# A selective scan's input products shared with GpSimd, and one ScalarE table for Exp and Ln

## Chip, core and metric

One NeuronCore of a Trainium2 chip. The time is that of one execution on the device, in microseconds (us).

## What is computed

Four images of 256 channels and 64 x 64 points go through four layers, each `x = x + layer(groupnorm(x))`: a deformable convolution, a self-attention, a second deformable convolution with groups, and a state-space layer (Mamba). The change is in the last one, layer 3, whose core is this (512 inner channels, 16 states, 4096 points in a row):

```python
delta = softplus(dt @ dt_proj_w.T + dt_proj_b)
deltaA = exp(delta * A)                 # A = -exp(A_log), per channel and state
deltaBu = delta * B * u                 # B per point and state
state = deltaA * state + deltaBu        # step by step along the points
y = sum over states of state * C        # C per point and state
out = ((y + u * D) * silu(res)) @ out_proj_w.T
```

## The kernel before

The images follow one another, each through layers 0 to 3. Layer 3 (`layer3`) cuts the 4096 points into 8 chunks of `C = 512`; the 512 channels lie in four groups (`dc`) of 128 partitions. A chunk has `DS = 16` states, so an image has 128 steps of the loop over `s`, with `j` the chunk and `n` the state. Everything is float32 but the two operands of `bn`.

One state:

- TensorE spreads row n of B over all partitions into PSUM (`bn`, L1396, one bank for all states).
- VectorE multiplies `du` (delta times u) by `bn`, 128 x 2048 elements, into `h` (L1468).
- ScalarE makes `da = exp(delta * A)` for each of the four groups (L1475, two PSUM banks), and VectorE runs the recurrence over it (L1476, four scans that start from `carry`).
- GpSimd saves the last column as `carry` (L1487) and multiplies `h` by row n of C (L1490). That row, `cn`, was spread over the partitions by a DMA from a small DRAM tile `cd` (L1394, six buffers).
- TensorE adds `h` into `y` with a unit matrix (`add`, L1388), two states later.

Beside the states of one chunk, the next chunk is prepared by `front(j)`: normalised input `xn` (L1222 on ScalarE, L1220 on GpSimd for chunk 1), projections into `up` (L1190, L1194), the short convolution (`convolve`, L1236 and L1241) into `u`, the Silus of `u` and of the gates (L1250, L1206), the shares dt, B, C (L1259, `dbc` at L1263, `cd` at L1266), the softplus (L1274, Abs and Relu at L1280 and L1281, Exp at L1287, Ln at L1303, additions on GpSimd at L1296, L1305, L1306, and `du` at L1307). `close` projects the finished chunk and stores it. All projections and convolutions share one PSUM bank (`front`).

The order of TensorE, ScalarE, VectorE and GpSimd is written out by hand. Each piece of `front` has a step and a half; `front(j)` runs with step 0 at state 12 of chunk j-2 (`LEAD = 4`), so that chunk j's convolutions fall into states 14, 15, 0 and 1 and its Silus into state 2; `front(1)` runs two states later, in chunk 0. `fill` puts a piece's matmuls on TensorE's queue, `empty` the rest on ScalarE's and GpSimd's. The end of a state's step in the loop:

```python
                    empty(s, 2)
                    if s + 1 < total:
                        state((s + 1) // DS, (s + 1) % DS)
                    late.append((j, n, h))
                    if len(late) > 2:
                        add(*late.pop(0))
                    fill(s + 1, 0)
```

So on TensorE's queue `bn` of the next state stands behind the second half's piece and ahead of the `y` products. SP, which issues the DMAs, is not in the hand-written order. ScalarE's table loads are placed by the compiler ahead of a function that the loaded set does not hold.

`first` prepares chunk 0 of an image alone, ahead of the loop. The whole code, cut to what the change touches:

Of the kernel before, what the change touches and what calls it, by code (L numbers as in the profile page):

```python
# [9 lines left out]
F32 = mybir.dt.float32  # L10
I32 = mybir.dt.int32
BF16 = mybir.dt.bfloat16
AF = mybir.ActivationFunctionType
# [3 lines left out]
P = 128  # L17
# [11 lines left out]
DS = 16  # L29
# [34 lines left out]
class Net:  # L64
# [993 lines left out]
    def layer3(self, x, out, nxt, early):  # L1058
# [2 lines left out]

        nc, tc = self.nc, self.tc
        C = 512
        NC, LEAD = N // C, 4
        with (
# [17 lines left out]
            pick = pa.tile([P, DS, P], BF16, tag="pickn", name="pickn")  # L1085
# [8 lines left out]
            tail = pa.tile([P, 4, 3], F32, tag="tail", name="tail")  # L1094
            nc.gpsimd.memset(tail, 0.0)
            kept = pa.tile([P, 2, C], F32, tag="kept", name="kept")
            tiny = pa.tile([P, 1], F32, tag="tiny", name="tiny")
            chunks = [{} for _ in range(NC)]

            def bank():  # L1100
                return self.psum.tile([P, C], F32, tag="ps", name="front")

            def first():


                c = chunks[0]
                spare = lambda: py.tile([P, C], F32, tag="y", name="front")
                xn = pa.tile([P, 2, C], F32, tag="xn3", name="xn3")
                for ct in range(2):
                    nc.vector.tensor_scalar(  # L1110
                        xn[:, ct, :], x[:, ct, :C], rs[:, ct : ct + 1], shift[:, ct : ct + 1], ALU.mult, ALU.add
                    )
                up = pa.tile([P, 4, C + 3], F32, tag="up", name="up")
                nc.gpsimd.tensor_copy(up[:, :, 0:3], tail)
                u, delta, du, w = (
                    pool.tile([P, 4, C], F32, tag=n, name=n)
                    for pool, n in ((pb, "u"), (pb, "delta"), (pb, "du"), (pa, "w3"))
                )
                c.update(u=u, delta=delta, du=du)

                def project(dc):
                    pu = spare()
                    for ct in range(2):
                        nc.tensor.matmul(pu, win[:, ct, bass.ts(dc, P)], xn[:, ct, :], start=(ct == 0), stop=(ct == 1))
                    nc.vector.tensor_copy(up[:, dc, 3:], pu)

                def convolve(dc):
                    cv = spare()
                    for i in range(4):
                        nc.tensor.matmul(cv, conv[:, dc, i, :], up[:, dc, i : i + C], start=(i == 0), stop=(i == 3))  # L1130
                    nc.scalar.activation(u[:, dc, :], cv, AF.Silu, bias=cb[:, dc : dc + 1])

                project(0)
                project(1)
                convolve(0)
                project(2)
                convolve(1)
                project(3)
                nc.gpsimd.tensor_copy(tail, up[:, :, C : C + 3])
                convolve(2)  # L1140
                convolve(3)
                px = bank()
                for dc in range(4):
                    nc.tensor.matmul(px, xpw[:, dc, :], u[:, dc, :], start=(dc == 0), stop=(dc == 3))
                nc.scalar.activation(tiny, self.eps, AF.Exp)
                dbc = pa.tile([P, C], F32, tag="dbc", name="dbc")
                nc.scalar.copy(dbc, px)
                c["cd"] = self.dram.tile([DS, C], F32, tag="cd", name="cd")
                nc.sync.dma_start(out=c["cd"], in_=dbc[16:32, :])
                pzs = []  # L1150
                for dc in range(4):
                    pzs.append(spare())
                    nc.tensor.matmul(pzs[dc], dtw[:, bass.ts(dc, P)], dbc, start=True, stop=True)

                c["gates"] = [spare() for _ in range(4)]
                for dc, pg in enumerate(c["gates"]):
                    for ct in range(2):
                        nc.tensor.matmul(
                            pg, win[:, ct, bass.ts(4 + dc, P)], xn[:, ct, :], start=(ct == 0), stop=(ct == 1)
                        )  # L1160
                bp, t = c["bp"], _ = (
                    pb.tile([P, C], BF16, tag="bp", name="bp"),
                    pa.tile([P, C], BF16, tag="bt", name="bt"),
                )
                for lo, hi in ((0, 64), (64, 96), (96, 128)):
                    nc.gpsimd.tensor_copy(bp[lo:hi], dbc[lo:hi])
                    if hi < P:
                        nc.gpsimd.tensor_copy(t[hi:], dbc[hi:])
                        nc.gpsimd.tensor_sub(dbc[hi:], dbc[hi:], t[hi:])
                for dc in range(4):  # L1170
                    nc.scalar.activation(w[:, dc, :], pzs[dc], AF.Abs, bias=dtb[:, dc : dc + 1])
                    nc.scalar.activation(du[:, dc, :], w[:, dc, :], AF.Exp, scale=-1.0)
                    nc.vector.tensor_scalar(delta[:, dc, :], pzs[dc], dtb[:, dc : dc + 1], 0.0, ALU.add, ALU.max)
                    nc.vector.tensor_scalar_add(w[:, dc, :], du[:, dc, :], 1.0)
                    nc.vector.scalar_tensor_tensor(
                        du[:, dc, :], w[:, dc, :], -1.0, du[:, dc, :], ALU.add, ALU.subtract
                    )
                    nc.vector.tensor_sub(delta[:, dc, :], delta[:, dc, :], du[:, dc, :])
                for dc in range(4):
                    nc.scalar.activation(w[:, dc, :], w[:, dc, :], AF.Ln)  # L1180
                    nc.vector.tensor_add(delta[:, dc, :], delta[:, dc, :], w[:, dc, :])
                    nc.vector.tensor_mul(du[:, dc, :], delta[:, dc, :], u[:, dc, :])
# [21 lines left out]
            def gate_silu(j):  # L1204
                sres = chunks[j]["sres"]
                nc.scalar.activation(sres, sres, AF.Silu)  # L1206

            def front(j):


                c = chunks[j]
# [37 lines left out]
                def silu():  # L1249
                    nc.scalar.activation(c["u"], c["u"], AF.Silu)  # L1250
                    gate_silu(j - 1)

                put(6, 0, None, silu)

# [6 lines left out]
                def keep():  # L1261
                    c["dbc"] = pa.tile([P, C], F32, tag="dbc", name="dbc")
                    nc.scalar.copy(c["dbc"], c["b"])  # L1263

                    c["cd"] = self.dram.tile([DS, C], F32, tag="cd", name="cd")
                    nc.sync.dma_start(out=c["cd"], in_=c["dbc"][16:32, :])  # L1266

                put(7, 1, shares, keep)

# [34 lines left out]
                last = 17 if j > 1 else 15  # L1304
# [82 lines left out]
                for dc in range(4):  # L1387
                    nc.tensor.matmul(c["ys"][dc], self.ident, h[:, dc, :], start=False, stop=(n == DS - 1))  # L1388

            def state(j, n):  # L1390

                c = chunks[j]
                cn = c["cn", n] = pb.tile([P, 1, C], F32, tag="cn", name="cn", bufs=6)
                nc.sync.dma_start(out=cn, in_=c["cd"][n : n + 1, :].unsqueeze(0).to_broadcast([P, 1, C]))  # L1394
                bn = c["bn", n] = pbb.tile([P, 1, C], F32, tag="bn", name="bn")
                nc.tensor.matmul(bn[:, 0, :], pick[:, n, :], c["bp"], start=True, stop=True)  # L1396


            slots = {}
# [10 lines left out]
                    slots.setdefault((DS * (j + 1) + step, half), []).append((pe, rest))  # L1410
            last = DS * (NC - 1)
            slots.setdefault((last, 0), []).append((None, keep))
            slots.setdefault((last + 2, 0), []).append((None, lambda: gate_silu(NC - 1)))
            slots.setdefault((last + 2, -1), []).append((None, lambda: fetch(NC - 1)))
            slots.setdefault((last + 5, -1), []).append((None, lambda: count(NC - 1)))
            for i in range(2):
# [30 lines left out]
            with tc.manual_schedule(  # L1447
# [8 lines left out]
                for pe, rest in begin:  # L1456
                    if pe:
                        pe()
                    rest()
                state(0, 0)  # L1460
                fill(0, 0)
                late = []
                total = NC * DS
                for s in range(total):
                    j, n = s // DS, s % DS
                    c = chunks[j]
                    h = pb.tile([P, 4, C], F32, tag="h", name="h", bufs=4)
                    nc.vector.tensor_mul(h, c["du"], c.pop(("bn", n)).to_broadcast([P, 4, C]))  # L1468
                    empty(s, -1)
                    if j and n == 2:  # L1470
                        gated(j - 1)
# [1 line left out]
                    def scan(dc):  # L1473
                        da = pda.tile([P, C], F32, tag="da", name="da")
                        nc.scalar.activation(da, c["delta"][:, dc, :], AF.Exp, scale=al[:, dc, n : n + 1])  # L1475
                        nc.vector.tensor_tensor_scan(  # L1476
                            h[:, dc, :], da, h[:, dc, :], carry[:, dc, n : n + 1], ALU.mult, ALU.add
                        )

                    scan(0)  # L1480
                    scan(1)
                    empty(s, 0)
                    fill(s, 1)
                    scan(2)
# [7 lines left out]
                        nc.vector.tensor_mul(h[:, 0:2, :], h[:, 0:2, :], cn.to_broadcast([P, 2, C]))  # L1492
                        nc.gpsimd.tensor_mul(h[:, 2:4, :], h[:, 2:4, :], cn.to_broadcast([P, 2, C]))
                    empty(s, 2)
                    if s + 1 < total:
                        state((s + 1) // DS, (s + 1) % DS)
                    late.append((j, n, h))
                    if len(late) > 2:
                        add(*late.pop(0))
# [131 lines left out]
```

## Time and profile before

| what | us |
|---|---|
| median of three runs (lowest, highest) | 10109.86 (10098.28, 10119.21) |
| the profiled execution | 10144.41 |
| its span, first to last instruction | 10142.6 |
| TensorE busy in the span | 8738.3 (86%) |
| VectorE busy | 7651.8 (75%) |
| GpSimd busy | 6768.8 (67%) |
| ScalarE busy | 4961.6 (49%) |
| layer 3 of image 0, first product of a state to the last | 1614.6 to 2565.8 |

The shares are means over four different layers; a layer-3 stretch of the trace has to be read by itself. In a group of instructions the columns are: line, engine, operation, output and inputs with their shapes, count, then busy time and mean ns of one, then the idle time of the engine just before them with what ended it. PE is TensorE, PEld its weight loads, DVE VectorE, ACT ScalarE, POOL GpSimd. A float32 matrix product shows as two matmuls.

### The profile page before, as it was taken

To read this page: it belongs to the slowest core of one execution; us is meant where nothing else is said; L and a number is where in the kernel's file an instruction comes from. 1 tells how busy PE (TensorE), PEld (TensorE's weight loads), DVE (VectorE), ACT (ScalarE), POOL (GpSimd) and SP (SyncE) were. 2 spreads that over 40 slices of the span, in tenths; PEclk is the share of its full clock that TensorE was granted. 3 is DMA by queue.
4 is the path that set the end of the run, shared out by engine and by line. 5 is a ranking of instruction groups with operands and counts; after the bars stand their busy time and mean duration, and the time that the engine had idled before them with its cause. 6 is when DMAs were issued, how large, how long until landed. Compare 5 with 4: busy or idle time off the path is not lost.

```text
span 10142.6 us, 88824 instructions
## 1 busy us (share of the span) xinstructions
PE 8738.3 (86%) x29189; PEld 4281.7 (42%) x29193; DVE 7651.8 (75%) x8215; ACT 4961.6 (49%) x7588; POOL 6768.8 (67%) x3952
## 2 busy tenths in 40 slices
PE   5789898998678989899877898989986789998997
PEld 3643343333464334333346434433334643443333
DVE  5764497999676459799967545889995754688998
ACT  3743334665474333566557333266645733326664
POOL 3646686787474668688757366768865736677886
PEclk9889999999899999999989999999998999999999
DMA  7830011111783001111178201111118810111111
GB/s 263 310 137 1 25 49 39 44 45 48 259 312 119 1 29 49 38 44 47 45 287 323 78 1 36 51 38 44 44 43 316 308 62 1 38 49 38 40 40 34
DMA packets 377891, 956.56 MB, mean 94 GB/s; under 512 B 34675, under 2 KB 107820, under 8 KB 375372
## 3 DMA queue, kind: packets, MB, share of 16 engines
q0 software_dynamic: 165888, 604.05, 16.6%
q1 hardware_dynamic: 211532, 346.73, 10.8%
q8 instruction: 234, 3.83, 0.2%
q14 instruction: 237, 1.94, 0.1%
HBM read 784.59 MB, written 92.32 MB: 86 GB/s over the span
## 4 chain that ended last, share of the span: by engine, by line
PE 24%; DVE 9%; ACT 5%; issue 4%; POOL 4%; DMA 3%; another core or an unknown queue 1%; SPq 0%; POOLq 0%; DVEq 0%; ACTq 0%
PE cx L555 5%; DVE h L1476 4%; PE pacc L840 3%; PE y L1388 2%; DMA g<-tab,idx 2%; PE pm L455 2%; PE front L1236 2%; POOL h L1490 2%; DVE h L1468 2%; PE sc L531 2%; PE front L1190 1%; ACT da L1475 1%; DVE r L353 1%; POOL g L344 1%; DMA ring<-ring 1%
## 5 line engine op out<-in xcount | busy, mean ns | idle before, releaser
L1476 DVE TENSOR_TENSOR_SCAN h<-da,carry,h 128x512 f32<-128x512 f32 x2048 | 2470.6, 1264 | 140.9 <-ACT da L1475 92.5
L1490 POOL TENSOR_TENSOR h<-h,cn 128x2048 f32<-128x2048 f32 x508 | 2300.0, 4527 | 41.1 <-POOL carry L1487 0.4
L1475 ACT ACTIVATE da<-delta,l3a 128x512 f32<-128x512 f32 x2048 | 1388.6, 689 | 1152.5 <-DVE h L1476 1150.7
L1388 PE MATMUL y<-h,ident 128*128 128x512 f32 x4096 | 1931.4, 616 | 4.5 <-POOL h L1490 3.5
L344 POOL DMA_INDIRECT g<-tab,idx x1152 | 1363.3, 1183 | 791.1 <-issue 362.8
L548 POOL TENSOR_TENSOR acc<-acc,e 128x1024 f32<-128x1024 f32 x480 | 1125.1, 2344 | 540.4 <-ACT e L544 519.7
L388 PE MATMUL pz<-cols,l0w 128*128 128x256 f32 x4608 | 1217.5, 411 | 219.8 <-ACT cols L377 95.8
L1388 PEld LDWEIGHTS y<-h,ident 128*128 128x128 f32 x4096 | 810.2, 198 | 1279.3 <-issue 1209.7
L353 DVE SCALAR_TENSOR_TENSOR r<-g,wx,r 128x512 f32<-128x512 f32 x1152 | 858.1, 745 | 434.3 <-ACT r L352 321.9
L1468 DVE TENSOR_TENSOR h<-du,bn 128x2048 f32<-128x2048 f32 x512 | 1157.9, 2262 | 26.3 <-PE front L1190 14.2
L465 DVE TENSOR_REDUCE m<-pm 128x3 f32<-128x1536 f32 (+1 forms) x372 | 602.3, 1625 | 716.9 <-PE pm L455 715.2
L388 PEld LDWEIGHTS pz<-cols,l0w 128*128 128x128 f32 x4608 | 896.9, 205 | 390.7 <-ACT cols L377 100.9
L823 DVE TENSOR_TENSOR prod<-ring,A 128x1280 f32<-128x1280 f32 x640 | 922.4, 1480 | 122.7 <-DMA ring<-ring 102.7
L555 PE MATMUL cx<-e,v 128*128 128x512 f32 x2048 | 1001.4, 616 | 0.0
L544 ACT ACTIVATE e<-sc 128x1024 f32<-128x1024 f32 x512 | 496.0, 1020 | 1032.4 <-PE sc L531 1032.4
L352 ACT ACTIVATE r<-g,wx 128x512 f32<-128x512 f32 x1152 | 826.6, 718 | 270.0 <-DMA g<-tab,idx 219.2
L840 PE MATMUL pacc<-prod,ident 128*128 128x512 f32 x1920 | 915.3, 610 | 37.7 <-DVE prod L823 23.7
L832 POOL TENSOR_TENSOR prod<-prod 128x512 f32<-128x512 f32 x640 | 800.3, 1274 | 187.8 <-DVE prod L823 170.1
L370 PE MATMUL pt<-ident,acc 128*128 128x128 f32 x2304 | 430.9, 295 | 304.9 <-DVE acc L361 200.7
L1487 POOL COPY carry<-h 128x4 f32<-128x4 f32 x512 | 98.0, 191 | 807.4 <-DVE h L1476 797.6
L555 PEld LDWEIGHTS cx<-e,v 128*128 128x128 f32 x2048 | 352.2, 189 | 598.8 <-issue 596.3
L360 ACT ACTIVATE acc<-r,wy 128x256 f32<-128x256 f32 x1152 | 571.4, 496 | 28.0 <-DVE r L353 22.4
(250 smaller groups left out, 11138.0 us busy)
## 6 DMA issues: line engine op xcount, KB each, us to landing
cn<-cd SPq DMA_DIRECT2D x512, 256.0 KB
tab<-vt SPq DMA_DIRECT2D x112, 640.0 KB
ring<-ring SPq DMA_DIRECT2D x288, 126.0 KB
ring<-ring SPq DMA_DIRECT2D x288, 124.0 KB
g<-tab,idx POOLq DMA_INDIRECT x1152
x<-in_x SPq DMA_DIRECT2D x64, 256.0 KB
out<-x SPq DMA_DIRECT2D x56, 256.0 KB
l0w<-in_l0w SPq DMA_DIRECT2D x4, 2304.0 KB
```

The lines of the kernel that those rows point to most:

```text
L344: nc.gpsimd.indirect_dma_start(out=g[:], out_offset=None, in_=tab[:, :], in_offset=bass.IndirectOffsetOnAxis(ap=idx[:, t, k : k + 1], axis=0),
L353: nc.vector.scalar_tensor_tensor(r, g[:, :, 1, :], wx[:, 1, t, k : k + 1], r, ALU.mult, ALU.add)
L388: nc.tensor.matmul(sums[m][:, ot, :256], wf[:, i, bass.ts(ot, P)], cols[m][:, i, :], start=(i == 0), stop=(i == 17),)
L548: nc.gpsimd.tensor_add(b["acc"], b["acc"], e)
L555: nc.tensor.matmul(blocks[qb]["cx"], v[:, 4 * (i + kt // 4 * 4) + kt % 4, :], e[:, bass.ts(i % 2, 512)], start=(kt == 0 and i == 0), stop= ...
L823: nc.vector.tensor_mul(d["prod"][:, :, t, :].rearrange("p x (g c) -> p x g c", c=GC), ring[y // VR % 4][:, :, y % VR, :].rearrange("p x (g ...
L840: nc.tensor.matmul(d["pd"], self.ident, prod[:, wx, :], start=(wy == 0 and wx == 4), stop=(wy == WIN - 1 and wx == 2),)
L1388: nc.tensor.matmul(c["ys"][dc], self.ident, h[:, dc, :], start=False, stop=(n == DS - 1))
L1468: nc.vector.tensor_mul(h, c["du"], c.pop(("bn", n)).to_broadcast([P, 4, C]))
L1475: nc.scalar.activation(da, c["delta"][:, dc, :], AF.Exp, scale=al[:, dc, n : n + 1])
L1476: nc.vector.tensor_tensor_scan(h[:, dc, :], da, h[:, dc, :], carry[:, dc, n : n + 1], ALU.mult, ALU.add)
L1490: nc.gpsimd.tensor_mul(h, h, cn.to_broadcast([P, 4, C]))
```

## The change

Three things. In states 14, 15 and 0 to 5 the fourth group's product `du * B` is made by GpSimd, a state ahead (`quarter`), from a row of B that a DMA spreads into SBUF (`bs`, two buffers); VectorE's product covers three groups there. For this `cd` holds the rows of C and of B, and `ahead` issues the loads two states ahead, `cn` with four buffers in place of six. `bn` is still made for all states. And ScalarE loads the table set that holds Exp and Ln by name (`tables`), once in `first` and after each pair of Silus.

```diff
@@ first @@
-                nc.scalar.activation(tiny, self.eps, AF.Exp)
+                tables()
...
-                c["cd"] = self.dram.tile([DS, C], F32, tag="cd", name="cd")
-                nc.sync.dma_start(out=c["cd"], in_=dbc[16:32, :])
+                c["cd"] = self.dram.tile([2 * DS, C], F32, tag="cd", name="cd")
+                nc.sync.dma_start(out=c["cd"], in_=dbc[16:48, :])
@@ front: silu, keep (cd as above) @@
                     gate_silu(j - 1)
+                    tables()
@@ layer3 @@
+            def tables():
+                nc.scalar.preload_act_table_set("natural_log_exp_and_others")
...
-            def state(j, n):
-                c = chunks[j]
-                cn = c["cn", n] = pb.tile([P, 1, C], F32, tag="cn", name="cn", bufs=6)
-                nc.sync.dma_start(out=cn, in_=c["cd"][n : n + 1, :].unsqueeze(0).to_broadcast([P, 1, C]))
-                bn = c["bn", n] = pbb.tile([P, 1, C], F32, tag="bn", name="bn")
-                nc.tensor.matmul(bn[:, 0, :], pick[:, n, :], c["bp"], start=True, stop=True)
+            hs, helped = {}, (14, 15, 0, 1, 2, 3, 4, 5)
+            def ahead(s):
+                if s < NC * DS:
+                    j, n = s // DS, s % DS
+                    c = chunks[j]
+                    for name, r, bufs in (("cn", n, 4), ("bs", DS + n, 2)):
+                        if name == "cn" or n in helped:
+                            t = c[name, n] = pb.tile([P, 1, C], F32, tag=name, name=name, bufs=bufs)
+                            nc.sync.dma_start(
+                                out=t, in_=c["cd"][r : r + 1, :].unsqueeze(0).to_broadcast([P, 1, C])
+                            )
+            def state(s):
+                if s < NC * DS:
+                    c = chunks[s // DS]
+                    bn = c["bn", s % DS] = pbb.tile([P, 1, C], F32, tag="bn", name="bn")
+                    nc.tensor.matmul(bn[:, 0, :], pick[:, s % DS, :], c["bp"], start=True, stop=True)
+            def quarter(s):
+                if s < NC * DS:
+                    c = chunks[s // DS]
+                    hs[s] = pb.tile([P, 4, C], F32, tag="h", name="h", bufs=4)
+                    if s % DS in helped:
+                        nc.gpsimd.tensor_mul(hs[s][:, 3:4, :], c["du"][:, 3:4, :], c.pop(("bs", s % DS)))
...
-            slots.setdefault((last + 2, 0), []).append((None, lambda: gate_silu(NC - 1)))
+            slots.setdefault((last + 2, 0), []).append((None, lambda: (gate_silu(NC - 1), tables())))
@@ the loop over states @@
-                state(0, 0)
+                for s in range(2):
+                    ahead(s)
+                state(0)
+                quarter(0)
...
-                    h = pb.tile([P, 4, C], F32, tag="h", name="h", bufs=4)
-                    nc.vector.tensor_mul(h, c["du"], c.pop(("bn", n)).to_broadcast([P, 4, C]))
+                    h = hs.pop(s)
+                    d = 3 if n in helped else 4
+                    nc.vector.tensor_mul(
+                        h[:, :d, :], c["du"][:, :d, :], c.pop(("bn", n)).to_broadcast([P, d, C])
+                    )
+                    ahead(s + 2)
...
                     scan(1)
+                    quarter(s + 1)
                     empty(s, 0)
...
-                    if s + 1 < total:
-                        state((s + 1) // DS, (s + 1) % DS)
+                    state(s + 1)
```

More of the change, by code (lines that the diff above doesn't have):

```diff
@@ L1096, in layer3 @@
             kept = pa.tile([P, 2, C], F32, tag="kept", name="kept")
-            tiny = pa.tile([P, 1], F32, tag="tiny", name="tiny")
             chunks = [{} for _ in range(NC)]
@@ L1263, in keep @@
                     nc.scalar.copy(c["dbc"], c["b"])
-                    c["cd"] = self.dram.tile([DS, C], F32, tag="cd", name="cd")
-                    nc.sync.dma_start(out=c["cd"], in_=c["dbc"][16:32, :])
+                    c["cd"] = self.dram.tile([2 * DS, C], F32, tag="cd", name="cd")
+                    nc.sync.dma_start(out=c["cd"], in_=c["dbc"][16:48, :])
                 put(7, 1, shares, keep)
```

## The prediction, made before the change was run

> **What bounds the kernel now.** I read the granted clock first (one core, 0.950 over the span), then the costliest groups on the page, to see what layer 3 is made of:
>
> ```profile
> L1476 DVE TENSOR_TENSOR_SCAN h<-da,carry,h 128x512 f32<-128x512 f32 x2048 | 2470.6, 1264 | 140.9 <-ACT da L1475 92.5
> L1490 POOL TENSOR_TENSOR h<-h,cn 128x2048 f32<-128x2048 f32 x508 | 2300.0, 4527 | 41.1 <-POOL carry L1487 0.4
> ...
> L1388 PE MATMUL y<-h,ident 128*128 128x512 f32 x4096 | 1931.4, 616 | 4.5 <-POOL h L1490 3.5
> ...
> L1468 DVE TENSOR_TENSOR h<-du,bn 128x2048 f32<-128x2048 f32 x512 | 1157.9, 2262 | 26.3 <-PE front L1190 14.2
> ```
>
> A state on VectorE is one product (2.26) and four scans (4.81 from first start to last end, and some 0.05 between): 7.09 us. VectorE is idle for only 26 us before 512 products and 141 us before 2048 scans, so a shorter product looks like a gain everywhere. The windows view asks who else is full. I cut a stretch of image 0 at the starts of VectorE's products; the rows are states 14 and 15 of chunk 2 (counted from 0), then 0 to 5 of chunk 3. Columns: stretch, length, busy time (count) of PE, weight loads, DVE, ACT, POOL, then granted clock, DMA share, GB/s.
>
> ```profile
> 1962.03:1969.60 7.57, 6.80 (x17) 2.86 (x16) 7.08 (x7) 2.95 (x5) 7.46 (x4) 1.00 0.21 67
> 1969.60:1976.71 7.11, 7.11 (x18) 3.13 (x17) 7.01 (x6) 3.29 (x6) 6.64 (x4) 1.00 0.02 4
> 1976.71:1983.80 7.09, 7.09 (x18) 3.13 (x17) 6.99 (x6) 3.27 (x6) 4.72 (x2) 1.00 0.21 66
> 1983.80:1990.89 7.09, 7.09 (x18) 3.13 (x17) 6.99 (x6) 3.27 (x6) 4.72 (x2) 1.00 0.16 32
> 1990.89:2001.88 10.99, 10.99 (x27) 4.85 (x26) 9.40 (x11) 9.82 (x10) 4.75 (x2) 1.00 0.11 33
> 2001.88:2008.96 7.08, 7.08 (x18) 2.94 (x16) 6.98 (x6) 3.25 (x5) 4.72 (x2) 1.00 0.11 30
> 2008.96:2016.05 7.09, 5.28 (x13) 2.21 (x13) 6.99 (x6) 4.80 (x8) 4.72 (x2) 1.00 0.12 40
> 2016.05:2023.14 7.09, 5.59 (x13) 2.01 (x12) 6.99 (x7) 5.02 (x9) 4.72 (x2) 1.00 0.14 36
> ```
>
> In states 15, 0 and 1 **TensorE is as full as VectorE**. A busy PE need not be at its peak, so I read the start times in the timeline:
>
> ```profile
> 1972.76 3.60 PE L1236 MATMUL front<-up,conv 128*128 128x512 f32 x8
> 1976.19 0.38 PE L1396 MATMUL bn<-bp,pickn 128*128 128x512 bf16 x1
> 1976.41 3.60 PE L1388 MATMUL y<-h,ident 128*128 128x512 f32 x8
> 1979.84 3.60 PE L1236 MATMUL front<-up,conv 128*128 128x512 f32 x8
> ```
>
> Eight matmuls take 3.43 from start to start, `bn` 0.22: 3.43 + 3.43 + 0.22 = 7.08 a state, back to back. `bn` of the next state stands behind the convolution; it starts at 1976.19, is over at 1976.57, and VectorE's product starts at 1976.71: 0.14 us of slack.
>
> State 2 ends on ScalarE:
>
> ```profile
> 1990.56 0.69 ACT L1241 ACTIVATE u<-front,l3b 128x512 f32<-128x512 f32 x1 [1.21 <-PE front L1236]
> 1991.15 1.29 ACT L1475 ACTIVATE da<-delta,l3a 128x512 f32<-128x512 f32 x2
> 1992.46 1.28 ACT L1250 ACT_TABLE_LOAD   x1
> 1993.75 1.91 ACT L1250 ACTIVATE u<-u 128x2048 f32<-128x2048 f32 x1
> 1995.57 1.89 ACT L1206 ACTIVATE sres<-sres 128x2048 f32<-128x2048 f32 x1
> 1997.48 1.28 ACT L1475 ACT_TABLE_LOAD   x1
> ...
> 1999.50 2.46 DVE L1476 TENSOR_TENSOR_SCAN h<-da,carry,h 128x512 f32<-128x512 f32 x2 [1.59 <-ACT da L1475]
> ```
>
> The last convolution releases `u`, two Silus and two table loads follow, and VectorE waits 1.59 us for `da`.
>
> **What the Trainium skill says.** "GPSIMD Engine Reference", section 1, Specifications: GpSimd's SBUF interfaces are shared with VectorE, with contention when VectorE runs a two-port mode or reads two SBUF inputs. The trace agrees: beside L1492, a VectorE product of two SBUF tiles, GpSimd's 1024 elements took 3384 ns against half of 4527; in the loop, where VectorE reads `bn` or `da` from PSUM, all 508 products lie between 4505 and 4571 ns. "ScalarE: Activation LUTs", sections "Table sets: the hidden batching unit" and "What ACT_TABLE_LOAD costs": the set natural_log_exp_and_others holds both functions, and a switch is 1283 ns and a drain of some 1380. The trace has the 1283, but the next activation starts 0.02 us later, so I price a switch at 1.28.
>
> **The change, part by part.**
>
> *Shorter product.* L1468 takes 2262 ns for 2048 elements, the like L1445 (PSUM by SBUF) 679 for 512: 1.03 ns an element, so 1536 take 1.73 and 0.53 is saved. 8 states x 8 chunks x 4 images x 0.53 = 136 us if nothing else held.
>
> - States 14, 15, 0, 1 between chunks j and j+1, for j = 0 to 5 (front(2) to front(7) convolve there). The chain runs from `xn` in state 12 (not helped) through TensorE and ScalarE's copies, then four full states. `bn` for states 15, 0, 1, 2 comes when it does now. The product of 15 already waits 0.39; the rest has 0.14 of slack. **Gain 0**: VectorE's wait on `bn` takes the place of the work.
> - State 2 there: `u` of the last convolution, the Silus, the second load (now in `tables()`, at the same place) are timed by TensorE. **Gain 0**; the wait for `da` grows from 1.59 to 2.12.
> - States 3, 4, 5 of chunks 1 to 6: `bn` is there some 4 us early (2004.91 for a product at 2008.96), because it stands ahead of the y products that keep TensorE full in state 3; then TensorE has 5.3 and ScalarE 5.0 to do in 6.56. Full gain, 3 x 0.53 = 1.60 a chunk.
> - States 14, 15 of chunk 6 and all eight of chunk 7 have no front (`bn` over 4 us early, no idle scan in state 2): 10 x 0.53 = 5.3 an image.
> - Chunk 0, with front(1) two states later: the first product waits for `bn` behind front(1)'s projections, unchanged. Without the load of 1614.99 the last `up` copy waits only for TensorE's projection; it and `bn` come 0.5 earlier, state 1 begins 0.4 earlier. Then convolutions and the y products of state 0 hold TensorE again, and Silu in state 4 follows them: 1.05 there. State 5 adds 0.53: 1.6 an image.
>
> *One table.* 64 loads at L1475, 28 at L1303, 4 at L1180 and 4 at L1145 go; 36 come with `tables()`: 164 loads in all become 100, 82 us less of ScalarE, nearly all hidden. The Silu pair stays. A pair around Ln (L1303, 2.56 us) costs VectorE a net 0.16 in state 9 (the stretch of 8.44 is 7.09 and 1.19 of statistics): 6 x 0.16 = 1.0 an image. In chunk 0, state 11, it waits 2.02 for it; the next front's `xn` is behind that on ScalarE, so its TensorE chain moves along: 2.0 an image. In first() the load and the dropped `tiny` stand in waits for TensorE and VectorE: nothing.
>
> *The quarter on GpSimd.* Four products of 2048 cost 4.53, and 64x512 at L1321 1.16; I take 1.16 for 128x512 (L832, in another layer and with a busy VectorE: 1.27). A helped state has 0.27 + 4.53 + 1.16 = 5.96 of 6.56. Tightest is state 15: GpSimd ends product 12 at 1962.2, then quarter 14 (1963.3), product 13 (1968.1), the next chunk's `du` (1972.6), quarter 15: 1973.8. Its scan is wanted at 1969.6 + 1.78 + 3.55 = 1974.9: 1.1 to spare. Its lag then shrinks, and y products have over 3 us. In chunk 0, where states 11 to 13 carry three additions in a row, quarter 15 is 0.7 late; the next states wait for `bn`, which hides that. Queued behind a late quarter are carry, `h` and then TensorE's y, two states later.
>
> *DMA.* 256 loads of `bs` more on SP, 0.32 us each to issue, and `cd` of 64 KB for 32. A `cn` of the same size lands 2.9 us after issue; `bs` of state s+2 is issued when quarter s ends and wanted some 12 us later. `cn` with 4 buffers waits for product s-2, still two states ahead. SP also stands behind output copies, waiting 1.0 us each. Cost 0, bounded at 0 to 1 us a chunk.
>
> *Sum for an image:* 6 x 1.60 + 5.3 + 1.6 + 1.0 + 2.0 = 19.5; four images 78 us. The profiled execution took 10144.4 (span 10142.6), 0.34% over the median of 10109.9: 10066 for a run like it, **10032 for the median**.
>
> **Rivals.**
>
> - *TensorE is no bound after all*, and all 256 products pay: 136 + 12 = 148, so 9962. For it: DVE has the larger share of layer 3 and its wait on `bn` totals only 12.0 us. Against: starts without a gap. Chance 0.05.
> - *GpSimd's lag eats the gain.* If a quarter takes 2.1, the 34 states an image that gain run at GpSimd's 6.90 and not 6.56 (0.34 x 34 x 4 = 46 lost); or the change doesn't do what it says and Exp loads its own set behind each `tables()` (1.28 x 28 = 36 in state 2, and the 12 of the Ln). Some 30 of 78 remain: 10080. Nothing shown speaks for it. Chance 0.08.
> - *GpSimd becomes the bound (slower).* Price from L1493: 3.4 for a quarter. Then GpSimd needs 8.2 a state; quarter 15 is 3.4 late, state 2 starts 5 late, the wait on Silu returns 3, and states 3 to 5 lose 1.1 each: some 5.6 a chunk, 150 in all: 10260. It decides from 1.8 a quarter on (6.56 - 0.27 - 4.53), and passes zero near 2.4. Against: GpSimd's times in the loop do not depend on VectorE. Chance 0.08, with lesser losses of the kind.
>
> **The numbers.** Forecast 0.79. The bounds of the unknown costs (quarter 1.13 to 1.27; SP 0 to 28 us) and runs that differ by 0.2% give 10002 to 10060; I extend the top to 10065 for the second rival. A measurement here tells 0.2%, some 20 us, from no change. Faster by more 0.87, within 0.05, slower 0.08.
>
> **What would show it.** L1468 splits into 256 of 2.26 and 256 of about 1.73; its wait on PE `bn` rises from 12 to some 60 us, at states 15, 0, 1, 2; the stretches of states 14 to 2 keep 7.57, 7.1, 7.1, 7.1, 11.0 while 3 to 5 become 6.56; the new GpSimd row has 256 of 1.16; no scan waits for it but once an image; state 11 of chunk 0 falls from 9.21 to about 7.1. I am wrong if states 14 to 1 get shorter, if scan 3 waits for GpSimd, or if a load stands before an Exp.

## The result and the profile after

The median fell from 10104.07 to 10025.76 us: ratio 0.9921, 95% interval 0.9904 to 0.9939; 78 us, and 78 was forecast (10032 against a before of 10109.9). The profiled execution of the changed kernel has a span of 10013.5, 129 less than that of before. From the first product of a state to the last, summed over the four images, layer 3's loop fell from 3806.1 to 3717.4, by 88.7; the other 40 us lie outside it. There only the preparation of chunk 0 was changed, and from its `xn` to the first product it took 50.9 us an image before and 50.9 to 51.6 after, so the 40 us are scatter: the time outside the loop runs from 6296 to 6360 us over the eleven profiled executions of this document. I compare loops below, since that scatter does not enter them. That both figures are 78 is chance, for the loop, which the forecast is about, gained 88.7, and a second series of the same two kernels (`after_again`) 100.

The page after, same columns as before:

```profile
L1510 DVE TENSOR_TENSOR_SCAN h<-da,carry,h 128x512 f32<-128x512 f32 x2048 | 2468.9, 1264 | 143.7 <-ACT da L1509 86.6
L1525 POOL TENSOR_TENSOR h<-h,cn 128x2048 f32<-128x2048 f32 x508 | 2299.8, 4527 | 41.0 <-POOL carry L1522 0.2
L1393 PE MATMUL y<-h,ident 128*128 128x512 f32 x4096 | 1913.8, 612 | 9.7 <-POOL h L1525 9.7
...
L1499 DVE TENSOR_TENSOR h<-du,bn 128x2048 f32<-128x2048 f32 (+1 forms) x512 | 1023.0, 1998 | 63.7 <-PE bn L1415 63.7
```

The products' busy time fell by 134.9. Their wait on `bn` reads 63.7, but it can't be set against the 12.0 of before as it stands. The list of groups before has it in two parts:

```profile
L1468 DVE TENSOR_TENSOR h<-du,bn 128x2048 f32<-128x2048 f32 x512 | 1157.9, 2262 | 26.3 <-PE front L1190 14.2 <-PE bn L1396 12.0
```

The 14.2 are the first product of each image, 3.56 us each. The profile of the changed kernel has the same 3.56 and puts them down to `bn`. Like for like, the wait on `bn` rose from 12.0 to 49.5. The groups by shape give the two lengths and the new one on GpSimd:

```profile
L1423 POOL TENSOR_TENSOR h<-du,bs 128x512 f32<-128x512 f32 x256 | 326.1, 1275 | 10.7 <-DVE du L1186 10.7
...
L1499 DVE TENSOR_TENSOR h<-du,bn 128x2048 f32<-128x2048 f32 x256 | 578.3, 2259 | 0.0
...
L1499 DVE TENSOR_TENSOR h<-du,bn 128x1536 f32<-128x1536 f32 x256 | 444.7, 1737 | 63.7 <-PE bn L1415 63.7
```

All waiting stands before the shorter products. It rose by 37.4 (26.3 to 63.7), so of the 134.9 saved 37.4 is waited again on `bn`, and some 12 more in state 2, where the wait for `da` grew. The windows view for the same states as in the prediction, 14 and 15 of chunk 2, then 0 to 5 of chunk 3 (image 0; length, then PE, weight loads, DVE, ACT, POOL):

```profile
1943.32:1950.81 7.49, 6.72 (x17) 2.86 (x16) 6.53 (x7) 2.79 (x5) 7.41 (x5) 1.00 0.38 80
1950.81:1957.89 7.08, 7.08 (x18) 3.13 (x17) 6.56 (x6) 3.26 (x6) 7.00 (x5) 1.00 0.31 65
1957.89:1964.98 7.09, 7.09 (x18) 3.13 (x17) 6.57 (x6) 3.27 (x6) 7.01 (x4) 1.00 0.25 75
1964.98:1972.06 7.08, 7.08 (x18) 3.13 (x17) 6.56 (x6) 3.26 (x6) 7.00 (x5) 1.00 0.24 74
1972.06:1983.16 11.10, 11.10 (x27) 4.85 (x26) 8.89 (x10) 9.93 (x10) 7.02 (x4) 1.00 0.37 95
1983.16:1989.72 6.56, 6.56 (x17) 2.95 (x16) 6.46 (x7) 3.25 (x5) 5.95 (x3) 1.00 0.05 18
1989.72:1996.27 6.55, 5.13 (x13) 2.10 (x12) 6.45 (x7) 4.89 (x8) 5.95 (x3) 1.00 0.35 89
1996.27:2002.82 6.55, 5.19 (x13) 2.10 (x12) 6.45 (x7) 5.02 (x9) 4.72 (x2) 1.00 0.28 73
```

States 14 to 2 add up to 39.84, before to 39.85. TensorE fills 15 to 2 from end to end, and VectorE now has some 0.5 us free in each of 15, 0 and 1. States 3 to 5 are 6.55 or 6.56.

### The profile page after: what moved, and what is told of

Read it like the earlier page. It is cut to its first block, busy times and chain, and to the rows that moved or that the text cites. A ratio compares the mean times of both kernels' runs of the same rounds, so it can differ in the third digit from the quotient of the medians.

```text
span 10013.5 us, 89698 instructions
## 1 busy us (share of the span) xinstructions
PE 8706.2 (87%) x29193; PEld 4277.9 (43%) x29193; DVE 7522.5 (75%) x8215; ACT 4882.2 (49%) x7520; POOL 7077.9 (71%) x4208
## 5 line engine op out<-in xcount | busy, mean ns | idle before, releaser
L1510 DVE TENSOR_TENSOR_SCAN h<-da,carry,h 128x512 f32<-128x512 f32 x2048 | 2468.9, 1264 | 143.7 <-ACT da L1509 86.6
L388 PE MATMUL pz<-cols,l0w 128*128 128x256 f32 x4608 | 1211.5, 410 | 183.8 <-DVE cols L377 94.2
L1499 DVE TENSOR_TENSOR h<-du,bn 128x2048 f32<-128x2048 f32 (+1 forms) x512 | 1023.0, 1998 | 63.7 <-PE bn L1415 63.7
L832 POOL TENSOR_TENSOR prod<-prod 128x512 f32<-128x512 f32 x640 | 800.9, 1276 | 187.2 <-DVE prod L823 166.4
L361 DVE SCALAR_TENSOR_TENSOR acc<-r,wy,acc 128x256 f32<-128x256 f32 x1152 | 548.7, 477 | 0.0
```

Source lines behind the costliest of these rows:

```text
L388: nc.tensor.matmul(sums[m][:, ot, :256], wf[:, i, bass.ts(ot, P)], cols[m][:, i, :], start=(i == 0), stop=(i == 17),)
L1499: nc.vector.tensor_mul(h[:, :d, :], c["du"][:, :d, :], c.pop(("bn", n)).to_broadcast([P, d, C]))
L1510: nc.vector.tensor_tensor_scan(h[:, dc, :], da, h[:, dc, :], carry[:, dc, n : n + 1], ALU.mult, ALU.add)
```

## The experiments

Each ratio is against runs of the kernel before that were made beside it. Loop times are of one profiled execution each; the two of the changed kernel (`after_again` is the same kernel) differ by 0.8. Table loads counted by line fell from 164 to 100 as reckoned.

| kernel | ratio to before (95%) | loop of layer 3, us | against before |
|---|---|---|---|
| before | 1 | 3806.1 | |
| changed | 0.9921 (0.9904 to 0.9939) | 3717.4 | -88.7 |
| after_again | 0.9903 (0.9888 to 0.9917) | 3716.6 | -89.5 |
| table_only | 0.9967 (0.9955 to 0.9980) | 3775.4 | -30.7 |
| quarter_only | 0.9939 (0.9926 to 0.9952) | 3742.6 | -63.5 |
| only_3_4_5 | 0.9930 (0.9915 to 0.9944) | 3732.5 | -73.6 |
| half_y_before | 0.9968 (0.9955 to 0.9980) | 3769.7 | -36.4 |
| half_y_after | 0.9842 (0.9829 to 0.9856) | 3638.4 | -167.7 |
| bn_first | 1.0057 (1.0044 to 1.0071) | 3871.1 | +65.0 |
| u_after_exps | 0.9895 (0.9881 to 0.9910) | 3698.6 | -107.5 |
| u_late_chunk7 | 0.9889 (0.9874 to 0.9904) | 3683.7 | -122.4 |

**The two parts, each alone.**

```diff
 # table_only: the kernel before with
+            def tables():
+                nc.scalar.preload_act_table_set("natural_log_exp_and_others")
 # and its calls; quarter_only: the changed kernel with
-                nc.scalar.preload_act_table_set("natural_log_exp_and_others")
+                pass
```

> The kernel before with tables() alone: one named table set, no product on GpSimd. What the two traces show of the tables: state 9 loses 1.36 us where no statistics stand beside the Ln (8.45 to 7.09: 6 chunks of image 3, chunk 1 of the others) and 0.36 elsewhere (15 chunks), state 11 of chunk 0 loses 2.1 in each image, and the start of chunk 0 some 0.5. Theory A (parts add up, and the tables' share is larger than the prediction's 12 us): 9 x 1.36 + 15 x 0.36 + 4 x 2.6 = 28 us faster, ratio 0.9972; bn waits as before (12 us). Rival (the tables are worth the 12 us of the prediction and the shorter product the rest): 0.9988.

> The kernel with the quarter on GpSimd, but the compiler places the table loads as before (Exp, then Ln, then Exp). Theory A: states 3 to 5 of chunks 1 to 6, states 14 and 15 of chunk 6 and all eight of chunk 7 pay 0.53 each, the start of chunk 0 some 1: (28 x 0.53 + 1) x 4 = 63 us faster, ratio 0.9938; wait of the product on bn about 63 us, states 14 to 2 unchanged. Rival (all 256 products pay): 136 us, 0.9865.

Measured: 30.7 and 63.5 us of the loop, theory A in each. Together they make 94.2 against 88.7 for both; in the changed kernel state 9 of chunk 0 reads 9.10 to 9.43 in three images, in table_only 7.77 in all four, and why was not looked into. The rival of the first (12 us, 0.9988) and of the second (136 us, 0.9865) lie outside the intervals. In quarter_only the stretch from state 14 to state 2 reads 39.82 on average between chunks 1 and 6, and the wait on `bn` is 48.7, with another 18.5 for the first products under `front`; the 63 of the expectation had the first products in it.

**Where the quarter pays.**

```diff
-            hs, helped = {}, (14, 15, 0, 1, 2, 3, 4, 5)
+            hs, helped = {}, (3, 4, 5)
```

> The changed kernel with GpSimd's quarter in states 3, 4 and 5 only. Theory A: states 14, 15, 0, 1, 2 pay only where no next chunk is convolved, which is states 14, 15 of chunk 6 and 14, 15, 0, 1, 2 of chunk 7 (7 x 0.53 an image) and some 0.7 at the start of chunk 0: 4.4 x 4 = 18 us slower than the changed kernel, ratio to before about 0.994; the stretch from state 14 to state 2 in chunks 1 to 6 is 39.8 us in both. Rival (each helped product pays alike): five eighths of the quarter's share of some 60 us are lost, 38 us slower than the changed kernel, 0.996.

The loop is 15.1 us longer than the changed kernel's, near the 18 and far from the 38. State 2 reads 10.98 with a whole product and, from chunk 2 on, 11.10 with three quarters of one; the stretch from 14 to 2 is 40.07 on average here and 39.98 in the changed kernel. So five of the eight helped states are worth something only where no next chunk is convolved.

**Is it TensorE?** Both kernels, with half of the y additions left out:

```diff
-                for dc in range(4):
+                for dc in range(4 if n == DS - 1 else 2):
                     nc.tensor.matmul(c["ys"][dc], self.ident, h[:, dc, :], start=False, stop=(n == DS - 1))
```

> The kernel before with half of TensorE's y additions left out (groups 2 and 3 are added in state 15 alone), so that TensorE has some 5.4 us a state to do where the next chunk is convolved instead of 7.08. Theory A: VectorE's period of 7.09 stays, the product of state 15 no longer waits for bn, and the Silu chain of state 2 starts about 1 us earlier: some 1.4 us a chunk, 24 times, 34 us faster than the kernel before, ratio 0.9966. Rival (TensorE is no limit): same as before.

> The changed kernel with the same y additions left out. Theory A (TensorE holds states 14 to 1 of six chunks): those four states now fall to about 6.56 as well, while state 2 stays with ScalarE's Silus: 24 x 4 x 0.53 = 51 us more than between the two kernels with all additions, so 130 us faster than half_y_before, ratio to before about 0.984. Rival (these states are held by something other than TensorE's work): again about 80 us between the pair, ratio 0.989, and the wait on bn stays near 60 us.

half_y_before is 36.4 us below the kernel before, where 34 was expected, and its stretch from 14 to 2 is 38.61. The pair differs by 131.3 us of the loop (9981.5 against 10113.8 in the medians: 132), where the full kernels differ by 89: the quarter's gain comes back when TensorE has less to do. The stretch falls from 38.61 to 36.50, which is four times 0.53. The same states 14 to 2 in half_y_after:

```profile
1948.34:1954.90 6.56, 5.79 (x15) 2.48 (x14) 6.46 (x6) 3.73 (x6) 6.48 (x5) 1.00 0.32 80
1954.90:1961.46 6.56, 6.56 (x17) 2.84 (x16) 6.46 (x6) 3.43 (x6) 6.48 (x5) 1.00 0.20 47
1961.46:1968.02 6.56, 6.16 (x15) 2.30 (x14) 6.46 (x7) 3.26 (x5) 6.48 (x4) 1.00 0.38 80
1968.02:1974.57 6.55, 6.55 (x16) 2.58 (x15) 6.45 (x6) 3.26 (x5) 6.47 (x4) 1.00 0.47 93
1974.57:1984.82 10.25, 8.42 (x21) 3.56 (x20) 8.87 (x11) 8.96 (x8) 9.51 (x5) 1.00 0.25 77
```

All four states are VectorE's 6.56, and the wait on `bn` in this kernel is 0.8 us in all, the first products apart. The PE column alone would mislead: TensorE is still full in two of the rows. The timeline tells why:

```profile
1955.56 3.60 PE L1240 MATMUL front<-up,conv 128*128 128x512 f32 x8
...
1960.93 3.60 PE L1240 MATMUL front<-up,conv 128*128 128x512 f32 x8
...
1976.36 0.38 PE L1415 MATMUL bn<-bp,pickn 128*128 128x512 bf16 x1 [1.60 <-DVE h L1499]
```

The convolutions start 5.37 apart, not 7.08: TensorE runs ahead of VectorE, and in state 2 it is the one that waits, 1.60 us. GpSimd too has next to no gap in these states, 7.00 of 7.08 in the changed kernel and 6.48 of 6.56 here, since it catches up after the next chunk's `du`. But its products start 5.97 apart in both kernels, and with the same GpSimd work the states here run at 6.56, so it isn't what holds the changed kernel. State 2 is 10.25 in this kernel and 10.24 in half_y_before: it stays with ScalarE's chain and gains nothing from a shorter product.

**Is it bn's place in the queue, or the work?**

```diff
                     empty(s, 0)
+                    state(s + 1)
                     fill(s, 1)
...
-                    state(s + 1)
```

> The changed kernel with bn of the next state queued on TensorE ahead of the second half's piece (the convolution) instead of behind it. Theory A (states 14 to 2 are held by the sum of TensorE's work up to the last convolution, and state 2 by the Silus behind it): the product no longer waits for bn (63 us fall to some 10) and states 14, 15, 0, 1 read about 6.6, but the last convolution comes no earlier, so the wait for da in state 2 grows by the same 2 us: 14 to 2 stays at 39.8, total as the changed kernel, 0.991. Rival B (the place of bn in the queue is the cause): 24 x 4 x 0.53 = 51 us faster than the changed kernel, 0.986.

The wait on `bn` fell from 63.7 to 21.3, of which 18.5 are the first products of the images: like for like from 49.5 to 2.8. States 14 to 2 came to 40.2 (6.81, 6.88, 7.08, 7.08, 12.37), so they gained nothing from a `bn` that comes early, and rival B falls. Theory A's 6.6 did not come in states 0 and 1. There ScalarE's copy of the convolution waits for TensorE, the exponentials stand behind that copy, and VectorE waits for `da` instead (ScalarE, then VectorE):

```profile
1979.01 0.69 ACT L1245 ACTIVATE u<-front,l3b 128x512 f32<-128x512 f32 x1 [2.60 <-PE front L1240]
1979.60 1.29 ACT L1509 ACTIVATE da<-delta,l3a 128x512 f32<-128x512 f32 x2
...
1980.31 4.81 DVE L1510 TENSOR_TENSOR_SCAN h<-da,carry,h 128x512 f32<-128x512 f32 x4 [0.63 <-ACT da L1509]
```

And the total missed both forecasts: 154 us of the loop more than the changed kernel. Most of it lies in states 4, 8 and 10, which read 8.94, 8.28 and 8.88 on average in chunks 1 to 6 against 6.56, 7.38 and 7.11. The timeline in chunk 3, states 3 and 4, shows why (PE rows, then ScalarE, then VectorE):

```profile
1999.19 0.58 PE L1415 MATMUL bn<-bp,pickn 128*128 128x512 bf16 x1 [2.62 <-DVE h L1499]
1999.57 4.97 PE L1264 MATMUL front<-u,l3b 128*128 128x512 f32 x8
...
2010.08 1.30 ACT L1509 ACTIVATE da<-delta,l3a 128x512 f32<-128x512 f32 x2
...
2010.81 2.46 DVE L1510 TENSOR_TENSOR_SCAN h<-da,carry,h 128x512 f32<-128x512 f32 x2 [2.56 <-ACT da L1509]
```

`bn` has one bank. Placed early it waits 2.62 us for VectorE to read the last one. The shares behind it start 2.16 us after state 3's product, in the changed kernel 0.78 before it. ScalarE stands at the copies of those shares (2.15 us here) and of the steps after them, and `da` is queued behind; before the first copy of each step, L1285, ScalarE is idle for 120 us in the whole run, in the changed kernel for 16. In states 8 and 10 of the same chunk it stands 3.17 and 3.27 at copies of the output and of a gate. VectorE's wait on `da` rose from 86.6 to 269.8 us in the whole run.

**State 2.** Here the copy of the last convolution goes behind two exponentials:

```diff
-                for dc in range(4):
+                late_pe, late_rest = convolve(3)
+                for dc in range(3):
                     put(2 + dc, 1, *convolve(dc))
+                put(5, 1, late_pe, lambda: None)
                 def silu():
+                    late_rest()
                     nc.scalar.activation(c["u"], c["u"], AF.Silu)
```

> The changed kernel with one move: ScalarE's copy of the last convolution (dc = 3) is queued behind the first two exponentials of state 2 instead of ahead of them, so that these run while TensorE still convolves. Theory A (state 2 is timed by the chain last convolution, u, two exponentials, load, two Silus, load, exponential): the chain has one exponential pair less after u, but the second exponential needs the last scan of state 1: 0.85 us less in state 2, 24 times: 20 us faster than the changed kernel, ratio to before about 0.990. Rival (state 2 is bound by VectorE or by the product of TensorE behind it): no difference from the changed kernel (0.992).

First the changed kernel in state 2 (ScalarE, then VectorE), then u_after_exps:

```profile
1971.84 0.69 ACT L1245 ACTIVATE u<-front,l3b 128x512 f32<-128x512 f32 x1 [1.82 <-PE front L1240]
1972.42 1.29 ACT L1509 ACTIVATE da<-delta,l3a 128x512 f32<-128x512 f32 x2
1973.73 1.28 ACT L1254 ACT_TABLE_LOAD   x1
...
1980.78 2.46 DVE L1510 TENSOR_TENSOR_SCAN h<-da,carry,h 128x512 f32<-128x512 f32 x2 [2.21 <-ACT da L1509]
```

```profile
1978.49 0.69 ACT L1512 ACTIVATE da<-delta,l3a 128x512 f32<-128x512 f32 x1 [0.48 <-DVE h L1513]
1979.12 0.67 ACT L1245 ACTIVATE u<-front,l3b 128x512 f32<-128x512 f32 x1
1979.81 1.28 ACT L1257 ACT_TABLE_LOAD   x1
...
1986.85 2.46 DVE L1513 TENSOR_TENSOR_SCAN h<-da,carry,h 128x512 f32<-128x512 f32 x2 [1.46 <-ACT da L1512]
```

ScalarE no longer stands 1.82 us at TensorE, the wait for `da` falls from 2.21 to 1.46, and state 2 reads 10.35 for 11.10 in chunks 2 to 6. The loop is 19 us shorter than the changed kernel's, where 20 was expected; the medians' ratios (0.9895 and 0.9903) can't tell that. With the quarter in all of chunk 7 as well:

```diff
-                    if s % DS in helped:
+                    if s % DS in helped or s // DS == NC - 1:
 # and the same in ahead and for d
```

> The changed kernel with u of the last convolution behind two exponentials (as in u_after_exps) and the quarter on GpSimd in all sixteen states of chunk 7, where no next chunk asks GpSimd for additions. Theory A: 0.75 us in state 2, 20 times, and 8 x 0.53 x 4 = 17 us in chunk 7: 30 us faster than the changed kernel, ratio to before 0.9875; states 6 to 13 of chunk 7 fall from 7.09 to 6.56 (statistics apart). Rival (states 7 and 9, with the output's projection on TensorE, wait for bn): 0.5 us less gained in each, 0.988; GpSimd's late quarters: scan 3 waits for GpSimd in chunk 7.

The loop is 34 us below the changed kernel's; states 6, 7 and 8 of chunk 7 read 6.55 or 6.56, so neither `bn` nor GpSimd is in the way. It is the fastest whole kernel here: 0.9889. Its interval still overlaps that of after_again, so that it beats the changed kernel rests on the traces' loops.

## Why the prediction was right

The mechanism held: the shorter product pays only where neither TensorE nor ScalarE sets the pace. Three sizes did not hold: the wait on `bn`, the loads around Ln, and the time of a quarter.

- **"Gain 0" in states 14 to 1:** held; the stretch to state 2 between chunks 1 and 6 of all images is 39.98 on average, before 39.84, the difference being a state 14 of 7.79 or 8.31 in some chunks. Such states come in table_only and only_3_4_5 too and not in quarter_only, so they go with the tables; their cause wasn't looked into. That TensorE's work holds these states is shown by the pair with half of the additions.
- **Wait on `bn`, "some 60":** 63.7 on the page looks like a hit, but 14.2 of it was there before under another name. Like for like it is 49.5. The forecast's own terms, 12 and in 24 chunks 0.53 for state 15 and 0.39 (0.53 less the slack of 0.14) for 0, 1 and 2, add up to 53: it seems to have left the slack out of the total. In chunks 2 to 6 states 0, 1 and 2 wait 0.42 each.
- **State 2, gain 0, wait 1.59 to 2.12:** 2.21 in chunks 2 to 6, where the state grew from 10.98 to 11.10.
- **States 3 to 5, and those of chunks 6 and 7:** 0.53 each, as forecast; states 14 and 15 of chunk 6 read 6.55.
- **Start of chunk 0:** 46.46 to 44.93 for states 0 to 5, 1.5 for 1.6. State 11 there: 9.21 to 7.09.
- **Mis-sized: the pair of loads around Ln in state 9.** I took 0.16 us for each of six chunks, from a state in which VectorE has 1.19 of statistics to do meanwhile, 1.0 an image. Without statistics the wait is open, as in image 3 of the kernel before (ScalarE, then VectorE):

```profile
9348.63 1.28 ACT L1303 ACT_TABLE_LOAD   x1
9349.93 1.91 ACT L1303 ACTIVATE w<-w 128x2048 f32<-128x2048 f32 x1
9351.86 1.28 ACT L1475 ACT_TABLE_LOAD   x1
9353.15 1.30 ACT L1475 ACTIVATE da<-delta,l3a 128x512 f32<-128x512 f32 x2
...
9353.88 2.46 DVE L1476 TENSOR_TENSOR_SCAN h<-da,carry,h 128x512 f32<-128x512 f32 x2 [1.25 <-ACT da L1475]
```

  This state went from 8.45 to 7.09, nine such chunks in four images, and the fifteen with statistics from 8.44 to 8.08: 17.6 us for the 4 of the forecast. Most of the 30.7 of table_only against the forecast's 12 is this. The 10.7 us by which the loop did better than 78 are the tables' 18.7 more than forecast, less some 2.5 that the quarter brought short of its 66 and the 5.5 by which the two together fall short of their sum.
- **Mis-sized, without effect: GpSimd.** A quarter takes 1.275, not 1.16. The 1.16 was measured on 64 partitions; the line of the same shape, L832 with 1.27, was at hand and set aside. In chunk 0 quarter 15 was 2.58 to 2.62 late in three of the four images, not 0.7. In quarter_only it was 0.85 to 0.92 late in all four: the rest came with the tables, which the forecast had reckoned apart. With both, VectorE's product of state 15 starts 2.3 us ahead of GpSimd's `du` in these images, in quarter_only 0.5 to 0.6. In the timeline (GpSimd, then VectorE's scan 3 of state 15 and its wait in state 2):

```profile
1718.82 4.51 POOL L1312 TENSOR_TENSOR du<-delta,u 128x2048 f32<-128x2048 f32 x1
1723.28 1.28 POOL L1423 TENSOR_TENSOR h<-du,bs 128x512 f32<-128x512 f32 x1
...
1724.59 1.28 DVE L1510 TENSOR_TENSOR_SCAN h<-da,carry,h 128x512 f32<-128x512 f32 x1 [2.58 <-POOL h L1423]
...
1746.77 2.46 DVE L1510 TENSOR_TENSOR_SCAN h<-da,carry,h 128x512 f32<-128x512 f32 x2 [1.38 <-ACT da L1509]
```

  The next states ran at 6.56, and the wait in state 2 was 1.38 and not 2.21: most was absorbed there. No other scan waited for GpSimd. "GpSimd becomes the bound" had no ground: all 256 quarters lie between 1.257 and 1.295, and the 3.4 of that rival was the time of 1024 elements, twice a quarter.
- **"The set is loaded again":** no Exp of layer 3 has a load any more.

## What to carry to other kernels

When one engine's work is shortened in a repeated step, add up the other engines' work in that step, state by state: here two engines had 7.09 and 7.08 us to do, and the wait counter that would have warned showed only 12 us in all. A wait that is covered by other work in the place one looks at may be open in the other images; read each distinct case before multiplying. The same wait can stand under two names in two pages; add all its names up before comparing. And moving an instruction ahead in an in-order queue also moves its wait ahead of all that stands behind it.

## What the runs showed that was not expected

The two kernels with fewer matmuls show a lower mean granted clock, 0.916 and 0.921, than the rest (0.949 to 0.953), while the stretches shown above read 1.00. What sets it wasn't tried.
